# Last unit of a two-layer attention kernel: x and projection weights loaded ahead of its attention, range verdict ahead of the last evictions, general path out of line

## The chip, the cores and the metric

The kernel runs on one core of one Trainium2 chip, the seven other cores idle. The metric is the device time of one execution in microseconds (us). Before the change it is 3362.7 us, the median of 3 runs (3362.5 to 3364.94). The profiled execution took 3362.13 us, and its first to last instruction span 3360.4 us; times of single instructions below count from the start of that span.

## The reference

Two attention blocks of the same form follow each other, on 8 images of 512 channels and 32 x 32 = 1024 positions. All data is float32. One block, cut to what matters:

```python
xn  = groupnorm(x) * gn_scale + gn_bias            # 8 groups in block 0, 32 in block 1
qkv = einsum('oc,bcn->bon', qkv_w, xn) + qkv_b
q, k, v = split(qkv, 3)                            # 8 heads of 64 channels each
attn = softmax(einsum('bhdi,bhdj->bhij', q, k) / sqrt(64))
out = einsum('bhij,bhdj->bhdi', attn, v)
return einsum('oc,bcn->bon', proj_w, out) + proj_b + x
```

## The kernel before

**Units.** The work is cut into 16 units, one for each pair of block and image: units 0 to 7 are block 0, units 8 to 15 block 1. A unit `u` has four stages. Its x is loaded into the single buffer `xn` and normalised there. `projections` makes q, k and v. `attention` runs 64 steps, for 4 pairs of heads x 2 halves of the queries x 8 tiles of keys. The output projection of the unit is not run at once: `project(old, ...)` of unit `u - 1` comes between the projections and the attention of unit `u`. The products of `projections` and `project` are made in seven block products in place of eight (`blocks`, in the manner of Strassen), whose left and right operands are mixed ahead by `mix_weights` and `mix_right`. The last unit has no later unit to go into; it is projected plainly by `project_last`.

**The order of the work** is the order in which it is written (`tc.manual_schedule()`): each engine runs its own instructions in program order, and waits for the data and buffers that an instruction needs. All loads and stores are issued from SyncE's queue (SPq in the profile), also in program order, so an issue that waits for its buffer holds up all issues behind it.

**Attention.** Each step makes scores in PSUM (L486, TensorE, PE for short), takes the exponential on ScalarE (ACT, L494) into one of four shared buffers `p`, and multiplies it with v (L514). VectorE (DVE) adds the exponentials up (L531, L533), transposes and reduces these sums (L546, L556), and three small transfers gather them as `lt` (L562). `reciprocals` then takes the reciprocal, writes it to device memory (`drec`, L584) and reads it back spread over the partitions (`rb`, L589). `divide` multiplies the attention output `ao` by `rb` (L596), and `add_bias` adds the bias of v on ACT (L603). The output `ao` has four parts of 128 channels, one for each pair of heads. The fourth part is the last to be complete: for it these steps come after the attention, as `rest`.

**Buffers.** The residual of a unit (`load_res`) goes to the four buffers `p`, which the exponentials also use. The tags `w0`, `w1` and `w2` hold the mixed q, k and v weights of the block at hand.

**The last projection**, `project_last` (L430 to L454). The outputs lie in eight groups `g` (4 parts of 128 output channels x 2 halves of the positions), one PSUM bank each, taken from `turns`. First all groups get their products over parts 0, 1 and 2 of `ao` (24 products, each recorded as two matmul instructions of 512 columns). Then come the parts `rest` that complete part 3. Then each group gets its product over part 3, its eviction with the residual on DVE (L451) and its store (L454). Before the change the residual and the plain weights are loaded just ahead of this call, L728 and L729.

**The range verdict** (L733 to L741). The fast path takes the exponential without the maximum of a row being subtracted. Whether that was safe is recorded on the way, in `okay` and `asum`. At the end four DVE operations bring this down to one value on each partition (`both`), a product with ones adds up over the partitions, and the integer `flag` is written. Every engine loads the flag (L951) and branches (L952): if it is below 128, `general_path` computes everything again in a slow and safe way. With the inputs at hand it isn't entered. After the branch, L993 holds the end of the program, where all engines meet.

Of the kernel before, what the change touches and what calls it, by code (L numbers as in the profile page):

```python
# [11 lines left out]
F32 = mybir.dt.float32  # L12
I32 = mybir.dt.int32
AF = mybir.ActivationFunctionType
ALU = mybir.AluOpType
AX = mybir.AxisListType
DEP = mybir.DependencyInfo(mybir.DependencyClass.Sync, mybir.DependencyReason.DATA)

P = 128
# [13 lines left out]
def fast_path(ctx, tc, x, qkv_wT, proj_wT, vecs, groups, out, flag):  # L33
# [14 lines left out]
    nc = tc.nc  # L48
    B, C, N = x.shape
    CC = C // P  # L50
# [10 lines left out]
    def pool(name, bufs, **kw):  # L61
        return ctx.enter_context(tc.tile_pool(name=name, bufs=bufs, **kw))

    const = pool("const", 1)
# [11 lines left out]
    small = pool("small", 2)  # L76
# [7 lines left out]
    abank = [apair[i // 2][:, i % 2, :] for i in range(4)]  # L84

    turns = [t[:, i, :] for i in range(2) for t in (*sbank, *apair)]
# [3 lines left out]
    ones = const.tile([P, H], F32, name="ones")  # L90
    half = const.tile([P, CC], F32, name="half")
    okay = const.tile([P, 2 * BL], F32, name="okay")
    asum = const.tile([P, 2 * B * CC], F32, name="asum")
# [12 lines left out]
    def load_x(u, tiles):  # L106
        l, b = units[u]
        src = x[b] if l == 0 else mid[b]
        for c in range(CC):
            nc.sync.dma_start(tiles[c], src[c * P : (c + 1) * P, :])  # L110

    def load_xn(u):
        t = xnpool.tile([P, CC, N], F32, tag="xn", name=f"xn_{u}")
        load_x(u, [t[:, c, :] for c in range(CC)])
        return t

    def load_res(u):
        tiles = [ppool.tile([P, N], F32, tag="p", name=f"x_{u}_{c}") for c in range(CC)]
        load_x(u, tiles)
        return tiles  # L120
# [11 lines left out]
    def mix_weights(l, mats, engine, first=0):  # L132


        lefts, parts = [], []
        add, sub = engine.tensor_add, engine.tensor_sub
        for i, a in enumerate(mats, first):
            a11, a12 = a[:, :2, :FD2], a[:, 2:, :FD2]
            a21, a22 = a[:, :2, FD2:], a[:, 2:, FD2:]
            s1, s2, s4 = (  # L140
                wpool.tile([P, 2, FD2], F32, tag=f"s{k}w{i}", name=f"s{k}w{i}_{l}")
                for k in (1, 2, 4)
            )
            parts += [
                partial(add, s1, a21, a22), partial(sub, s2, s1, a11),
                partial(sub, a21, a11, a21), partial(sub, s4, a12, s2),
            ]
            lefts.append({1: a11, 2: a12, 3: s4, 4: a22, 5: s1, 6: s2, 7: a21})
        return lefts, parts

    def mix_right(name, low, high):


        b11, b12 = low[:, :, :FD], low[:, :, FD:]
        b21, b22 = high[:, :, :FD], high[:, :, FD:]
        t1, t2, t4 = (
            tpool.tile([P, 2, FD], F32, tag=f"{name[0]}{k}", name=f"{name}_t{k}")
            for k in (1, 2, 4)
        )
        sub = nc.vector.tensor_sub  # L160
        parts = (
            partial(sub, t1, b12, b11), partial(sub, t2, b22, t1),
            partial(sub, t4, b21, t2), partial(sub, b12, b22, b12),
        )
        return {1: b11, 2: b21, 3: b22, 4: t4, 5: t1, 6: t2, 7: b12}, parts

    def load_proj(l, tag):
        w = wpool.tile([P, CC, C], F32, tag=tag, name=f"wproj_{l}_{tag}")
        nc.sync.dma_start(w, proj_wT[l].rearrange("(c p) o -> p c o", p=P))
        return w  # L170
# [259 lines left out]
    def project_last(w, rest):  # L430

        l, b = units[w.u]
        dst = mid[b] if l == 0 else out[b]

        def products(g, c):
            o, h = divmod(g, NH)
            nc.tensor.matmul(  # L437
                turns[g], w.wproj[:, c, ts(o, P)], w.ao[c // 2][:, c % 2, ts(h, FD)],
                start=(c == 0), stop=(c == CC - 1),
            )  # L440

        for g in range(CC * NH):
            for c in range(CC - 1):
                products(g, c)
        for part in rest:
            part()
        for g in range(CC * NH):
            o, h = divmod(g, NH)
            products(g, CC - 1)
            cols = w.res[o][:, ts(h, FD)]  # L450
            nc.vector.scalar_tensor_tensor(  # L451
                cols, turns[g], vec[:, l, PB, o : o + 1], cols, ALU.add, ALU.add
            )
            nc.sync.dma_start(dst[o * P : (o + 1) * P, ts(h, FD)], cols)  # L454
# [205 lines left out]
    rest = {g: mixing_w[2 * i + 2 : 2 * i + 4] for i, g in enumerate((1, 3, 5, 8, 10))}  # L660
    rest[12] = mixing_o

    old = None
    for u in range(2 * B):
        w = Unit()
        w.u, w.right, w.lefts = u, right, lefts
        w.evac_before = []
        for part in mixing[2:]:
            part()
        if u == B + 1:  # L670
            rest[16] = mixing_o
        projections(w, rest)
        if old is not None:
            old.res = load_res(old.u)
        nxt = None
        if u + 1 < 2 * B:
            xn = load_xn(u + 1)
            nxt = norm_parts(u + 1, xn)
            right, mixing = mix_right(f"x_{u + 1}", xn[:, :2], xn[:, 2:])
        if u == B - 1:  # L680
            lefts, mixing_w = mix_weights(1, load_weights(1), nc.gpsimd)
            for part in mixing_w:
                part()

        def stats_of(*which):
            for i in which if nxt is not None else ():
                nxt[1](i // NH, i % NH)

        if old is not None:
            old.left = left_o  # L690
            stats_after = {3: (0, 1, 2), 4: (3,), 6: (4, 5), 7: (6, 7)}
            project(old, lambda g: stats_of(*stats_after.get(g, ())))
            w.evac_before = old.evac
            if old.u == B - 1:
                (left_o,), mixing_o = mix_weights(1, [load_proj(1, "wproj")], nc.vector, 3)


        late = 1 if u == 0 else 0

        def at_step(s, state):  # L700
            if nxt is None:
                return
            st, stats, aggregate, means, variances, scales, apply, _ = nxt
            c, t = divmod(s, NT)

            pair = (c + 1) % 2
            free = state["free"][pair]
            c -= late
            if u == 0 and NT // 2 <= s < NT:
                stats_of(2 * s - NT, 2 * s - NT + 1)  # L710
            if c == 1 and t == 1:
                aggregate()
            elif c == 1 and t == 3:
                means(abank[2 * pair], *free)
                free[:] = [st["last"]]
            elif c == 1 and t == 5:
                variances(abank[2 * pair], *free)
                free[:] = [st["last"]]
            elif c == 2 and t == 0:
                scales()  # L720
            elif 2 <= c < 2 + CC and t in (4, 6):
                apply(c - 2, int(t == 6))
            elif c == 2 + CC and t in (2, 5):
                mixing[int(t == 5)]()

        rest = attention(w, at_step)
        old = w
    old.res = load_res(old.u)  # L728
    old.wproj = load_proj(1, "w0")  # L729
    project_last(old, [part for g in (4, 10) for part in rest[g]])  # L730


    fin = small.tile([P, 2 * B * CC], F32, tag="fin", name="fin", bufs=1)  # L733
    nc.vector.tensor_scalar(fin, asum, 0.0, 0.0, ALU.mult, ALU.is_equal)
    low = small.tile([P, 2], F32, tag="low", name="low", bufs=1)
    nc.vector.tensor_reduce(low[:, 0:1], fin, AX.X, ALU.min)
    nc.vector.tensor_reduce(low[:, 1:2], okay, AX.X, ALU.min)
    both = small.tile([P, 1], F32, tag="both", name="both", bufs=1)
    nc.vector.tensor_mul(both, low[:, 0:1], low[:, 1:2])
    nc.tensor.matmul(abank[0][:1, :1], both, ones[:, :1], start=True, stop=True)  # L740
    nc.vector.tensor_copy(flag, abank[0][:1, :1])  # L741


def general_path(ctx, tc, x, qkv_wT, proj_wT, vecs, groups, out):
# [199 lines left out]
def attention_blocks_kernel(tc, x, qkv_wT, proj_wT, vecs, groups, out):  # L944
    nc = tc.nc
    with tc.tile_pool(name="flag", bufs=1) as keep:
        flag = keep.tile([1, 1], I32, name="flag")
        with ExitStack() as ctx:
            ctx.enter_context(tc.manual_schedule())
            fast_path(ctx, tc, x, qkv_wT, proj_wT, vecs, groups, out, flag)  # L950
        good = nc.values_load(flag[0:1, 0:1], min_val=0, max_val=P)  # L951
        with tc.If(good < P):  # L952
            with ExitStack() as ctx:
                general_path(ctx, tc, x, qkv_wT, proj_wT, vecs, groups, out)

# [49 lines left out]
```

## Time and profile before

| | |
|---|---|
| time, median of 3 | 3362.7 us |
| span of the profiled execution | 3360.4 us |
| PE busy (matmul) | 3316.9 us, 99% |
| VectorE busy | 2376.2 us, 71% |
| ScalarE busy | 1394.1 us, 41% |
| mean load on the memory | 44 GB/s |

How the stages around the change look, from the view that gives busy times by stretch:

| stretch, us from the start | what runs | PE busy | granted PE clock |
|---|---|---|---|
| 3098.2 to 3304.8 | last unit, up to the end of its attention | 206.59 | 1.00 |
| 3304.8 to 3322.8 | between attention and last projection | 0.01 | 0.57 |
| 3322.8 to 3345.9 | last projection, parts 0 to 2 | 23.10 | 0.89 |
| 3345.9 to 3353.0 | last projection, part 3 | 7.03 | 1.00 |
| 3353.0 to 3360.4 | verdict, branch, end | 0.19 | 0.63 |

The granted clock is the share of full speed that the chip gave TensorE. Busy time of PE is modelled from the ends of pipelined matmuls, so 99% doesn't say that its array is used at its peak. A row of the timeline or of the chain gives a start, a length and then the engine, the line of the kernel and the operation; what stands in brackets is how long the engine sat idle before it, and what released it. "SPq", "ACTq" and so on are the instruction queues of the engines, in which loads of registers, branches and semaphores show that don't count as busy.

### The profile page before, as it was taken

What the parts mean: (1) busy time and instruction counts of PE and PEld (TensorE: products, weight loads), DVE (VectorE), ACT (ScalarE), POOL (GpSimd) and SP (SyncE); (2) the same over time, 40 slices, a digit from 0 to 9 for tenths busy, and PEclk for the clock granted to TensorE, in tenths of its full rate; (3) what the DMA queues carried; (4) which work ended last, traced back from release to release, by engine and by line L of the source; (5) the groups of instructions that cost most, each with busy time, mean ns of one, the idle gap of its engine ahead of it and who ended that gap; (6) DMA issues with size and microseconds to landing.
All of it is one profiled execution on the core that took longest, in us unless ns stands there. A gap on an engine that the chain in (4) does not pass through costs nothing.

```text
span 3360.4 us, 51078 instructions
## 1 busy us (share of the span) xinstructions
PE 3316.9 (99%) x21002; PEld 1645.9 (49%) x21002; DVE 2376.2 (71%) x2978; ACT 1394.1 (41%) x1548; POOL 49.2 (1%) x32
## 2 busy tenths in 40 slices
PE   8999999999999999999999999999999999999996
PEld 4445454454545445454454544545445454454532
DVE  4876948668486785857859587594876948769484
ACT  1633606336172351724517154271542716336062
POOL 0000000000000000002000000000000000000000
PEclk9999999999999999999999999999999999999998
DMA  2011010110201111012120111101111010110102
GB/s 77 33 39 57 22 69 27 33 57 21 82 15 33 58 32 71 15 33 101 33 76 15 41 55 34 63 21 57 33 33 63 21 63 27 39 57 21 44 27 77
DMA packets 66845, 149.28 MB, mean 44 GB/s; under 512 B 20784, under 2 KB 21040, under 8 KB 66608
## 3 DMA queue, kind: packets, MB, share of 16 engines
q1 hardware_dynamic: 66608, 145.95, 13.1%
q8 instruction: 170, 2.79, 0.3%
q14 instruction: 67, 0.55, 0.1%
HBM read 110.26 MB, written 34.08 MB: 43 GB/s over the span
## 4 chain that ended last, share of the span: by engine, by line
PE 98%; DVE 1%; DMA 0%; issue 0%; SPq 0%; ACT 0%; POOL 0%; DVEq 0%
PE a L288 26%; PE a L514 26%; PE s L486 25%; PE s L288 19%; PE a L486 1%; PE s L437 0%; PE a L437 0%; DVE acc L533 0%; DMA wproj_w<-proj_wT_dram 0%; DMA xn<-x_dram 0%; DVE tr L546 0%; SPq L110 0%; PE a L196 0%; DVE red L556 0%; DVE acc L531 0%
## 5 line engine op out<-in xcount | busy, mean ns | idle before, releaser
L494 ACT ACTIVATE p<-s 128x1024 f32<-128x1024 f32 x976 | 998.3, 1024 | 815.8 <-PE s L486 781.8
L514 PE MATMUL a<-p,v 64*64 64x512 f32 x8192 | 1101.3, 589 | 0.1
L486 PE MATMUL s<-q,k 64*64 64x512 f32 x7808 | 1059.4, 590 | 1.4 <-DVE v L375 1.4
L533 DVE TENSOR_TENSOR acc<-acc,p 128x1024 f32<-128x1024 f32 x768 | 939.7, 1224 | 87.7 <-ACT p L494 39.6
L514 PEld LDWEIGHTS a<-p,v 64*64 64x64 f32 x8192 | 384.9, 131 | 494.4 <-ACT p L494 349.4
L486 PEld LDWEIGHTS s<-q,k 64*64 64x64 f32 x7808 | 385.8, 133 | 437.1 <-issue 434.6
L288 PE MATMUL a<-xn,w 128*128 128x512 f32 x512 | 233.4, 599 | 4.0 <-DVE xn L244 4.0
L531 DVE TENSOR_TENSOR acc<-p,p 128x1024 f32<-128x1024 f32 x128 | 153.7, 1201 | 12.9 <-ACT p L494 12.9
L288 PEld LDWEIGHTS a<-xn,w 128*128 128x128 f32 x512 | 96.6, 191 | 131.9 <-issue 127.4
L546 DVE STREAM_TRANSPOSE tr<-acc 128x1024 f32<-128x1024 f32 x128 | 158.0, 1235 | 0.0
L556 DVE TENSOR_REDUCE red<-tr 128x32 f32<-128x1024 f32 x128 | 153.9, 1202 | 0.6
L540 DVE TENSOR_TENSOR ao<-a,tmp 128x512 f32<-128x512 f32 x128 | 88.0, 688 | 68.8 <-ACT tmp L539 68.8
L300 ACT COPY p_k<-a 128x1024 f32<-128x1024 f32 x16 | 16.2, 1012 | 255.0 <-PE a L288 255.0
L300 ACT COPY p_o<-a 128x1024 f32<-128x1024 f32 x15 | 15.2, 1012 | 244.2 <-PE a L288 244.2
L288 PE MATMUL a<-w,xn 128*128 128x256 f32 x512 | 115.7, 379 | 0.0
L288 PE MATMUL s<-xn,w 128*128 128x512 f32 x256 | 115.2, 592 | 0.4 <-DVE u_q L304 0.4
L288 PE MATMUL s<-x_t,s2w 128*128 128x512 f32 x256 | 115.1, 592 | 0.0
L288 PE MATMUL a<-x_t,s1w 128*128 128x512 f32 x256 | 115.1, 592 | 0.0
L288 PE MATMUL s<-x_t,w 128*128 128x512 f32 x256 | 115.1, 592 | 0.0
L288 PE MATMUL a<-xn,s4w 128*128 128x512 f32 x256 | 115.1, 592 | 0.0
L300 ACT COPY p_v<-a 128x1024 f32<-128x1024 f32 x16 | 16.2, 1012 | 237.3 <-PE a L288 221.4
L288 PE MATMUL a<-ao,wproj_wproj 128*128 128x512 f32 x240 | 107.9, 592 | 0.0
(129 smaller groups left out, 2847.7 us busy)
## 6 DMA issues: line engine op xcount, KB each, us to landing
rb<-drec SPq DMA_DIRECT2D x128, 256.0 KB, 3.9
xn<-x_dram SPq DMA_DIRECT2D x32, 512.0 KB, 5.2
x<-x_dram SPq DMA_DIRECT2D x32, 512.0 KB, 4.6
mid<-x SPq DMA_DIRECT2D x64, 256.0 KB, 2.1
xn<-mid SPq DMA_DIRECT2D x32, 512.0 KB, 4.9
x<-mid SPq DMA_DIRECT2D x32, 512.0 KB, 5.0
out_dram<-x SPq DMA_DIRECT2D x64, 256.0 KB, 2.1
w<-qkv_wT_dram SPq DMA_DIRECT2D x6, 1024.0 KB, 11.5
```

The costliest lines, as they stand in the source:

```text
L288: nc.tensor.matmul(dst, at[:, c, ts(i, P)], moving[:, c, :], start=start and c == 0 and not (tokens and i % 2), stop=stop and c == 1, skip ...
L300: nc.scalar.copy(p1, bx)
L486: nc.tensor.matmul(bank[e * H : (e + 1) * H, j, :], w.k[pr][j * H : (j + 1) * H, t * P + e * H : t * P + (e + 1) * H], w.q[pr][j * H : (j ...
L494: exp = nc.scalar.activation(p, bank, AF.Exp, scale=SCALE)
L514: nc.tensor.matmul(banks[r][j * H : (j + 1) * H, :], w.v[rows, t, lo : lo + D], p[rows, j, :], start=(t == 0), stop=(t == NT - 1),)
L531: nc.vector.tensor_add(acc, state["first"], p)
L533: nc.vector.tensor_add(acc, acc, p)
L540: i1 = nc.vector.tensor_add(w.ao[pr // 2][:, pr % 2, ts(qh, FD)], banks[1], tmp)
L546: nc.vector.transpose(tr, state["acc"].pop(c))
L556: nc.vector.tensor_reduce(red[:, :, qh, :], state["tr"].rearrange("p j (f i) -> p j f i", i=BL), AX.X, ALU.add)
```

## The change

Three edits, all around the end of the kernel:

1. In the last unit there is no next x to load. Where other units load it, after their own projections, the last unit now loads its own x once more, into the same buffer `xn`, as the residual, and the plain projection weights into `w0`. The two loads ahead of `project_last` go.
2. The four DVE operations of the verdict become the last of the `rest` parts, ahead of the evictions of the last projection. The product with ones now goes to a bank of `turns`, and the flag is copied out by ScalarE instead of VectorE.
3. The branch on the flag is told that its body isn't the block to fall through to, so that the general path is laid out away from the straight path.

The aim is that PE finds its operands at the end of the attention, and that less is done in series after the last product.

```diff
             nxt = norm_parts(u + 1, xn)
             right, mixing = mix_right(f"x_{u + 1}", xn[:, :2], xn[:, 2:])
+        else:
+            again = load_xn(u)
+            w.res = [again[:, c, :] for c in range(CC)]
+            w.wproj = load_proj(1, "w0")
         if u == B - 1:
...
-    old.res = load_res(old.u)
-    old.wproj = load_proj(1, "w0")
-    project_last(old, [part for g in (4, 10) for part in rest[g]])
-
-    fin = small.tile([P, 2 * B * CC], F32, tag="fin", name="fin", bufs=1)
-    nc.vector.tensor_scalar(fin, asum, 0.0, 0.0, ALU.mult, ALU.is_equal)
-    low = small.tile([P, 2], F32, tag="low", name="low", bufs=1)
-    nc.vector.tensor_reduce(low[:, 0:1], fin, AX.X, ALU.min)
-    nc.vector.tensor_reduce(low[:, 1:2], okay, AX.X, ALU.min)
-    both = small.tile([P, 1], F32, tag="both", name="both", bufs=1)
-    nc.vector.tensor_mul(both, low[:, 0:1], low[:, 1:2])
-    nc.tensor.matmul(abank[0][:1, :1], both, ones[:, :1], start=True, stop=True)
-    nc.vector.tensor_copy(flag, abank[0][:1, :1])
+
+    both = const.tile([P, 1], F32, name="both")
+
+    def verdict():
+        fin = small.tile([P, 2 * B * CC], F32, tag="fin", name="fin", bufs=1)
+        nc.vector.tensor_scalar(fin, asum, 0.0, 0.0, ALU.mult, ALU.is_equal)
+        low = small.tile([P, 2], F32, tag="low", name="low", bufs=1)
+        nc.vector.tensor_reduce(low[:, 0:1], fin, AX.X, ALU.min)
+        nc.vector.tensor_reduce(low[:, 1:2], okay, AX.X, ALU.min)
+        nc.vector.tensor_mul(both, low[:, 0:1], low[:, 1:2])
+
+    project_last(old, [part for g in (4, 10) for part in rest[g]] + [verdict])
+    nc.tensor.matmul(turns[0][:1, :1], both, ones[:, :1], start=True, stop=True)
+    nc.scalar.copy(flag, turns[0][:1, :1])
...
-        with tc.If(good < P):
+        with tc.If(good < P, preferred_fallthrough_block=False):
```

## The prediction

> **What bounds the kernel now.** I read the page first, then the chain of waits. The page's chain puts the whole kernel on one engine:
>
> ```profile
> PE 98%; DVE 1%; DMA 0%; issue 0%; SPq 0%; ACT 0%; POOL 0%; DVEq 0%
> ```
>
> So an edit pays only where TensorE (PE) stands still, or after it has finished. The chain in order of time, asked for the last 65 us, has one such place; its columns are start, length (both us) and the piece:
>
> ```profile
> 3314.12 8.63 DMA wproj_w<-proj_wT_dram
> 3322.75 0.04 issue
> 3322.79 7.82 PE s L437 x12
> 3330.61 5.15 PE a L437 x12
> ```
>
> The last projection (L437) waits for a weight load that is issued when the attention is already over, and its first 12 matmul instructions take 7.82 us where the next 12 take 5.15. The timeline shows what the load queues behind and which work was ready long before:
>
> ```profile
> 3302.03 2.75 PE L514 MATMUL a<-p,v 64*64 64x512 f32 x24
> 3305.34 1.33 ACT L603 ACTIVATE ao<-ao,vec 128x512 f32<-128x512 f32 x2
> 3307.05 0.68 DVE L540 TENSOR_TENSOR ao<-a,tmp 128x512 f32<-128x512 f32 x1
> 3310.17 1.80 SPq L562 DMA_DIRECT2D lt<-red  x3
> 3312.08 1.94 SPq L110 DMA_DIRECT2D x<-mid  x4
> 3314.90 0.47 SPq L584 DMA_DIRECT2D drec<-rec  x1
> 3322.92 1.12 SPq L589 DMA_DIRECT2D rb<-drec  x2
> 3327.69 1.23 DVE L596 SCALAR_TENSOR_TENSOR ao<-ao,rb 128x1024 f32<-128x1024 f32 x1 [12.87 <-DMA rb<-drec]
> ```
>
> PE ends its attention products at 3304.78 and starts again at 3322.79: 18.0 us idle. On SyncE's queue (SPq) the x and weight loads stand behind the `lt` transfers of the denominators. `drec`, issued behind the weights at 3314.90, lands 8.0 us later (the page's DMA rows for all units: `rb` 3.9).
>
> The second place is after the last product, which ends at 3352.94. The flag is written at 3354.67 + 0.15 = 3354.82, but the span ends at 3360.4. The rows of the lines of the range test's branch (L952) and of the end (L993) give durations in ns and start times:
>
> ```profile
> L952 SPq EVENT_SEMAPHORE  x8: 17/17/17, 3356.2 to 3356.8; - x8
> L952 ACTq COMPARE_BRANCH  x1: 50/50/50, 3355.4 to 3355.4; - x1
> L952 PEldq COMPARE_BRANCH  x1: 3412/3412/3412, 3355.5 to 3355.5; - x1
> L952 ACTq EVENT_SEMAPHORE  x1: 17/17/17, 3358.9 to 3358.9; - x1
> L952 DVEq EVENT_SEMAPHORE  x1: 21/21/21, 3359.3 to 3359.3; - x1
> L993 SPq EVENT_SEMAPHORE  x10: 17/28/2254, 3356.8 to 3360.3; - x10
> ```
>
> PE sits 3.41 us in its branch; ScalarE (ACT) and VectorE (DVE) branch at 3355.4 and 3355.5 and do their next instruction at 3358.9 and 3359.3. SyncE, there at 3356.8, waits 2.25 us for them.
>
> [...] the first weight loads after the gap come 0.86 us apart, later ones 0.43; the price here is 7.82 − 5.15 = 2.67 us.
>
> **The change, part by part.**
>
> *Removed from the end: the x loads and the weight load.* The next thing PE can do after the attention is L437's first group. At the same place one unit earlier PE goes from its last x24 group at 3095.48 to 128*128 products at 3098.22, 2.74 us later, so the start becomes 3302.03 + 2.74 = 3304.77. Is its data there? The first four instructions (0.43 each) use `ao` parts finished long ago; the fifth, at 3306.49, needs the third part's bias, whose first half ends near 3305.34 + 0.66 = 3306.0. The second half and the `ao` of L540 (3307.73) are not needed before. This assumes waits by region, not by tile. At the start of the kernel, products on `xn` begin at 17.00 while other columns of `xn` are still written until 19.06, so regions it is. The start moves by 3322.79 − 3304.77 = 18.02 us, and with no idle window the 2.67 us of half clock go too: **20.7 us**. The 48 instructions then end at 3304.77 + 48 × 0.429 = 3325.4 (3346.06 before).
>
> *Does the last quarter wait instead?* Its chain starts with the `lt` transfers, unmoved. The third lands at 3313.18. Five small DVE operations follow, until 3314.5. `drec` goes out at once and takes 1.45 us with no weights ahead of it (mid-attention: issue 3268.37, `rb` issue 3269.82), so `rb` is issued at 3315.98. Issue to divide was 3327.69 − 3322.92 = 4.77, so divide runs 3320.75 to 3321.98 and the first half of the bias ends at about 3322.7. PE asks for it at 3325.4. Slack 2.7 us, cost nothing.
>
> *Added in the last unit: 2 MB of x and 1 MB of weights.* They stand on SPq behind the residual of the unit before. The x load needs the buffer `xn`, free when the V products end. The unit before does this with its own next load:
>
> ```profile
> 2964.03 1.75 SPq L110 DMA_DIRECT2D xn<-mid  x4
> 2975.11 14.60 SPq L411 DMA_DIRECT2D out_dram<-x  x8
> 3181.84 14.60 SPq L411 DMA_DIRECT2D out_dram<-x  x8
> ```
>
> The units are 3181.84 − 2975.11 = 206.73 apart, so x goes out at 3170.8, the weights at about 3172.6 for 0.69 us of issue; their buffer's last readers are the Q products (the first K product is already copied out at 3125.99). Queued behind them are the stores of L411, which begin at 3181.84; whoever needs those is the attention's exp, through the shared buffers. 3 MB at the 407 GB/s that the DMA view shows while the same loads run take 7.4 us, done near 3179, before the first store. Hidden behind 24 us of projection: nothing.
>
> *Verdict ahead of the evictions.* Four DVE operations (0.18 + 0.22 + 0.21 + 0.16) run at about 3322 to 3323, behind the divide, while DVE waits for PE: nothing. What waits behind them, the first eviction, needs a product of 3326.2. At the end there remain a matmul (0.20) and an ACT copy of one element; bounds for that are the DVE cast (0.15) and the ACT copy of 512 (0.58), I take 0.2.
>
> *Tail,* in before's clock. Flag at 3352.94 + 0.04 + 0.20 + 0.02 + 0.20 = 3353.4. DVE ends its last eviction at 3353.71, loads the flag (0.55) and branches by 3354.5. SyncE issues the last store until 3354.07 and takes 0.95 us for its flag load, check and branch as before (3354.8 to 3355.75): 3355.0. If the good path falls through, no engine fetches. Then the last store, issued 3353.73, lands 2.0 to 2.1 later, at 3355.8; SyncE's eight semaphore instructions cost 0 to 0.6 after it. From the last arrival to the end before took 3360.4 − 3359.3 = 1.1 us. New end: 3356.9 to 3357.5, **3.3 us** earlier (2.9 to 3.5).
>
> Sum: 20.7 + 3.3 = 24.0; 3362.7 − 24.0 = **3338.7 us**.
>
> **The rivals.**
>
> 1. *The fetch stays.* The new block order may only move the jump: a good path that is placed elsewhere, or must leap over the general path at the end. For it: the trace doesn't show the layout. Against: the name of the option says which side falls through. Then only the flag chain shortens: DVE branches at about 3354.4 in place of 3355.5, so 1.1 us in place of 3.3: 3362.7 − 20.7 − 1.1 = 3340.9.
> 2. *PE stops at the third part.* If the wait covers the whole `ao` tile, it lasts until L540, 3307.77 in place of 3306.49: 1.3 us, 3340.0. The regions at the start of the kernel speak against it.
> 3. *The denominator chain takes the weight load's place.* If it took 5 us more than worked out, the last quarter would wait 5 − 2.7 = 2.3 us: 3341.0. Without loads beside it, `rb` and `drec` have no reason to.
> 4. *Slower.* A buffer of the moved loads comes free only late in the last unit; SPq stands still, the stores behind go out late and the exps wait for their buffers. Held until the projection ends (3194.7), eight stores of 0.33 us and 2.1 of landing reach 3199.5, where the first exp started at 3195.85: some 4 us lost. With the weights also late, so that the 20.7 are not won, and a second fetch (3.4) on the way back from the moved block: 3362.7 + 4 + 3.4 = 3370. Unit 14's loads in the same place issue on time, which speaks against it.
>
> **Chances.** Forecast 0.68; fetch stays 0.18; third part 0.06; denominator chain 0.05; slower 0.02; within 0.2% (some 6.7 us) 0.01, since it needs most of the 18 us idle to survive. Faster 0.97. The range runs from the best tail with a microsecond of scatter, 3336.9, past rivals 1 to 3 to 3342.0.
>
> **What would show it.** Right: L437's first instruction within 2 us of 3304.8 and its first x12 near 5.2 us; no PE wait at the last quarter; PE's branch under 0.2 us; first store of the unit before still near 3181.8; span near 3336.4. Wrong: a PE wait for `ao` or for a DMA at L437, a branch of over 3 us on any engine, or an exp at 3196 that waits for a store.

## The result, and the profile after

The changed kernel takes 3341.79 us (median of 6 runs, 3340.12 to 3343.34) against 3362.94 us of the kernel before (6 runs). The ratio is 0.9936, with a 95% interval from 0.9923 to 0.9948: 21.2 us less, where 24.0 were forecast.

The profiled execution has a span of 3340.0 us, 20.4 less than before. The chain of waits of its last 50 us (start, length, piece) has no transfer in it any more:

```profile
3303.67 2.58 PE a L514 x24
3306.25 5.35 PE s L437 x12
3311.59 5.15 PE a L437 x12
...
3321.89 5.15 PE a L437 x12
3327.05 1.72 PE s L437 x4
...
3332.20 1.73 PE a L437 x4
```

The 8.63 us of the weight load have gone, and with them the first x12 of 7.82 us: it is 5.35 now. The timeline shows when the moved loads run, and that the denominators' chain has become free of them:

```profile
3172.22 1.75 SPq L110 DMA_DIRECT2D xn<-mid  x4
3174.06 0.49 SPq L169 DMA_DIRECT2D wproj_w<-proj_wT_dram  x1
3183.30 14.60 SPq L411 DMA_DIRECT2D out_dram<-x  x8
...
3303.49 2.75 PE L514 MATMUL a<-p,v 64*64 64x512 f32 x24
3306.18 5.42 PE L437 MATMUL s<-ao,wproj_w 128*128 128x512 f32 x12
3317.36 1.12 SPq L589 DMA_DIRECT2D rb<-drec  x2
3321.91 1.22 DVE L596 SCALAR_TENSOR_TENSOR ao<-ao,rb 128x1024 f32<-128x1024 f32 x1 [5.62 <-DMA rb<-drec]
3323.17 1.33 ACT L603 ACTIVATE ao<-ao,vec 128x512 f32<-128x512 f32 x2 [15.04 <-DVE ao L596]
```

The stores of the unit before begin 9.2 us after the weights are issued, with the same 14.60 us for the eight issues as before. Divide and bias are done before PE asks for the last quarter at 3326.88. The third part, too, is there in time. The first half of its bias (L603, 1.33 us for two) ends at about 3307.46 (estimate). PE's weight loads (PEld) of the first x12 go on in even steps across the one that waits for it, at 3307.57:

```profile
3306.80 1.33 ACT L603 ACTIVATE ao<-ao,vec 128x512 f32<-128x512 f32 x2
...
3307.14 0.19 PEld L437 LDWEIGHTS s<-ao,wproj_w 128*128 128x128 f32 x1 [0.24 <-issue]
3307.57 0.19 PEld L437 LDWEIGHTS s<-ao,wproj_w 128*128 128x128 f32 x1 [0.24 <-ACT ao L603]
3308.00 0.19 PEld L437 LDWEIGHTS s<-ao,wproj_w 128*128 128x128 f32 x1 [0.24 <-issue]
...
3308.51 0.68 DVE L540 TENSOR_TENSOR ao<-a,tmp 128x512 f32<-128x512 f32 x1
```

L540 writes another region of the same `ao` only later, and PE doesn't wait for that.

The branch (now L957) and the end (L998) look different from before, but not as forecast. Durations in ns, min/median/max, then first and last start:

```profile
L957 SPq EVENT_SEMAPHORE  x8: 17/17/17, 3336.1 to 3337.8; - x8
L957 ACTq COMPARE_BRANCH  x2: 38/44/49, 3334.8 to 3334.9; - x2
L957 PEldq COMPARE_BRANCH  x2: 95/1959/3823, 3334.8 to 3335.1; - x2
L957 DVEq COMPARE_BRANCH  x2: 51/55/59, 3334.9 to 3335.2; - x2
L957 SPq COMPARE_BRANCH  x2: 43/46/49, 3336.0 to 3337.9; - x2
L998 DVEq DRAIN  x2: 10/34/58, 3339.2 to 3339.6; - x2
```

Each engine now has two jumps. The first falls through (95 ns on PE). The second leads to the end of the program, over the general path, which still lies in between (the run with the short body below bears this out), and it takes PE 3.82 us, more than the 3.41 before. VectorE starts its second at 3335.2 and does its next instruction at 3339.2.

For comparisons two stretches are enough. **Stretch 1** goes from the start of the last x24 group of the attention to the end of the last product, **the tail** from there to the end of the span. Before: 3352.94 − 3302.03 = 50.91 and 3360.4 − 3352.94 = 7.46 us. After: 3333.93 − 3303.49 = 30.44 and 3340.0 − 3333.93 = 6.07 us. So stretch 1 gives 20.5 us and the tail 1.4, 21.9 together. That the profiled spans differ by 20.4 is due to 1.46 us that this execution lost long before the edits (the x24 group starts at 3303.49 in place of 3302.03); most of it, 1.04 us, went in its opening products, as the last section shows.

### The profile page after: what moved, and what is told of

It is laid out like the page before. It is cut to its first block, busy times and chain, and to the rows that moved or that the text cites. A ratio compares the mean times of both kernels' runs of the same rounds, so it can differ in the third digit from the quotient of the medians.

```text
span 3340.0 us, 51079 instructions
## 1 busy us (share of the span) xinstructions
PE 3315.5 (99%) x21002; PEld 1645.3 (49%) x21002; DVE 2375.6 (71%) x2977; ACT 1393.5 (42%) x1549; POOL 48.1 (1%) x32
## 4 chain that ended last, share of the span: by engine, by line
PE 98%; DVE 1%; issue 0%; DMA 0%; ACT 0%; POOL 0%; SPq 0%; DVEq 0%
PE a L514 26%; PE a L288 26%; PE s L486 25%; PE s L288 19%; PE a L486 1%; PE s L437 0%; PE a L437 0%; DMA xn<-x_dram 0%; DVE acc L533 0%; DVE x L422 0%; DVE stats L184 0%; PE a L196 0%; DVE tr L546 0%; DVE u_o L390 0%; POOL y L216 0%
## 5 line engine op out<-in xcount | busy, mean ns | idle before, releaser
L288 PE MATMUL a<-xn,w 128*128 128x512 f32 x512 | 234.4, 601 | 4.0 <-DVE xn L244 4.0
L288 PEld LDWEIGHTS a<-xn,w 128*128 128x128 f32 x512 | 96.9, 192 | 132.7 <-issue 128.1
L540 DVE TENSOR_TENSOR ao<-a,tmp 128x512 f32<-128x512 f32 x128 | 88.0, 687 | 69.9 <-ACT tmp L539 69.9
L300 ACT COPY p_o<-a 128x1024 f32<-128x1024 f32 x15 | 15.2, 1012 | 244.2 <-PE a L288 244.2
L288 PE MATMUL a<-w,xn 128*128 128x256 f32 x512 | 115.7, 379 | 0.0
L288 PE MATMUL s<-xn,w 128*128 128x512 f32 x256 | 115.2, 593 | 0.4 <-DVE u_q L304 0.4
L288 PE MATMUL s<-x_t,s2w 128*128 128x512 f32 x256 | 115.1, 592 | 0.0
L288 PE MATMUL a<-x_t,s1w 128*128 128x512 f32 x256 | 115.1, 592 | 0.0
L288 PE MATMUL s<-x_t,w 128*128 128x512 f32 x256 | 115.1, 592 | 0.0
L288 PE MATMUL a<-xn,s4w 128*128 128x512 f32 x256 | 115.1, 592 | 0.0
L288 PE MATMUL a<-ao,wproj_wproj 128*128 128x512 f32 x240 | 107.9, 592 | 0.0
```

The source lines that it names most:

```text
L288: nc.tensor.matmul(dst, at[:, c, ts(i, P)], moving[:, c, :], start=start and c == 0 and not (tokens and i % 2), stop=stop and c == 1, skip ...
L300: nc.scalar.copy(p1, bx)
L540: i1 = nc.vector.tensor_add(w.ao[pr // 2][:, pr % 2, ts(qh, FD)], banks[1], tmp)
```

## The experiments

Theory A, formed on this profile: the moved loads are nearly all of the gain, by an idle time and a half clock (granted 0.50 from 3323 to 3326 us before) that both go; the verdict gives about a microsecond; the layout only moves the jump, so that the end still waits for a far target. The rival B is the forecast: the layout takes the fetch away. Other rivals stand with each run. One table for all, each row from one profile and from the times of that kernel; each ratio is to the runs of the kernel before that stood beside it:

| kernel | stretch 1, us | tail, us | time, us | ratio to before, 95% interval |
|---|---|---|---|---|
| before | 50.91 | 7.46 | 3362.94 | |
| changed | 30.44 | 6.07 | 3341.79 | 0.9923 to 0.9948 |
| changed, once more | 30.44 | 6.20 | 3340.66 | 0.9917 to 0.9950 |
| loads only | 30.43 | 7.45 | 3342.44 | 0.9922 to 0.9955 |
| verdict only | 51.14 | 6.65 | 3362.09 | 0.9987 to 1.0005 |
| layout only | 51.22 | 7.57 | 3362.61 | 0.9990 to 1.0007 |
| changed without layout | 30.44 | 6.55 | 3341.08 | 0.9917 to 0.9950 |
| short body | 30.43 | 4.53 | 3338.88 | 0.9913 to 0.9946 |
| weights only early | 32.28 | 6.27 | 3343.48 | 0.9925 to 0.9958 |
| x only early | 45.59 | 6.30 | 3356.02 | 0.9970 to 0.9985 |
| before, PE kept busy | 48.34 | 8.14 | 3361.24 | 0.9985 to 1.0002 |
| hint | 30.43 | 6.57 | 3341.52 | 0.9919 to 0.9952 |
| block without hint | 30.43 | 6.56 | 3341.11 | 0.9917 to 0.9950 |
| late hint | 30.44 | 6.47 | 3341.70 | 0.9919 to 0.9953 |

The intervals are as wide as the effects of the two small edits, so those are judged by the tails of the profiles.

**One edit alone, and all but one.** The first three are the kernel before with one of the three edits of the diff above. Loads only:

> The first edit alone: x and projection weights of the last unit loaded ahead of its attention; verdict and branch as before. Theory A (the loads are nearly the whole gain, and the jump over the general path is only moved by the third edit): L437 starts 2.7 us after the last x24 attention group starts (20.8 us before), its first x12 takes 5.3 to 5.4 us, the tail from the last product to the end stays 7.5 us as before; in all 20.5 us less, about 3342.4 us. Theory B (as forecast, 3.3 of the gain belong to verdict and layout and the loads give 20.7): the same time for this run, since they differ only in the next three. Theory C (most of the idle time is replaced by another wait, for the bias or the denominators): a PE wait of several us at L437 and 3345 us or more.

Measured: L437 starts 2.69 us after the x24 group, stretch 1 is 30.43 and the tail 7.45. Expected by A and B; C, a new wait, is out. This edit alone is 20.5 us.

Verdict only:

> The second edit alone: four DVE operations of the verdict ahead of the last evictions, flag copied by ScalarE; loads late and branch as before. Theory A: the flag is written 1.4 us sooner after the last product (0.3 in place of 1.9 us), but VectorE is held by its last eviction and branches only 1.1 us sooner, so the tail shrinks from 7.5 to about 6.3 us and the time to 3361.7 us. Theory B: the same 1.1 us. Rival: the tail is set by the last store and doesn't move, 3362.9 us. The 18 us wait for the weights stays in every theory.

Measured: tail 6.65, so 0.8 in place of the 1.1 expected. The rows of its branch (L953) say why. VectorE branches at 3355.1, 1.05 us after the last product (3354.05) in place of 2.6, but then takes 4.6 us to its next instruction in place of 3.8; PE's jump too has become longer, 4.17 us:

```profile
L953 PEldq COMPARE_BRANCH  x1: 4172/4172/4172, 3355.0 to 3355.0; - x1
L953 DVEq COMPARE_BRANCH  x1: 76/76/76, 3355.1 to 3355.1; - x1
L953 DVEq EVENT_SEMAPHORE  x1: 21/21/21, 3359.7 to 3359.7; - x1
```

The last store also lands later there, 3.9 us after its issue in place of 2.1. Layout only:

> The third edit alone: general path not the block to fall through to; all else as before. Theory A (the branch on the flag now falls through, but is followed by a jump over the general path to the end, which waits for the same fetch): two branches on each engine, the second one of PE about 3.8 us long, VectorE and ScalarE reach the end 4 us after their jump, tail 7.5 to 7.9 us, time 3362.9 to 3363.3 us. Theory B (the fetch goes): no branch above 0.2 us, tail 5.3 us, time 3360.7 us.

Measured: two jumps on each engine, the second of PE 3.84 us; tail 7.57, no gain. B is out. The changed kernel without layout:

```diff
-        with tc.If(good < P, preferred_fallthrough_block=False):
+        with tc.If(good < P):
```

> The changed kernel without its third edit: loads and verdict moved, the general path in line again, so that the branch on the flag is taken. Theory A (the layout moves the jump and takes nothing away): one branch of about 3.4 us on PE, tail 5.9 to 6.3 us against 6.07 with the layout edit, time within 0.5 us of the changed kernel's 3341.8. Theory B (the layout edit still brings something): a tail of 7.5 us or more, 3343.5 us.

Measured: a jump of 4.25 us on PE, tail 6.55, slightly outside what A gave (5.9 to 6.3), far from B's 7.5. To see whether those 0.5 us are scatter, the changed kernel ran once more:

> The changed kernel once more, to see how far its tail of 6.07 us repeats, against 6.55 without the layout edit. If the layout edit brings half a microsecond together with the early verdict, the tail is again 6.0 to 6.2 us; if it was the scatter of one execution, it may lie at 6.3 to 6.7 us. The stretch from the last x24 group to the last product stays 30.4 us.

Its tail is 6.20. The four profiles with early verdict and the layout edit have 6.07, 6.20, 6.27 and 6.30 us, the three with early verdict and neither layout edit nor hint 6.55, 6.56 and 6.65. The groups don't overlap, so the layout edit seems to bring 0.3 to 0.4 us beside an early verdict; alone it brought none in the one profile (7.57 against 7.46). The times don't resolve it.

**Is the fetch what the tail waits for?** That a long jump waits for instructions to be fetched was the author's assumption in the prediction; the rows of the branch show only how long it takes. The general path replaced by two small transfers:

```diff
-                general_path(ctx, tc, x, qkv_wT, proj_wT, vecs, groups, out)
+                few = ctx.enter_context(tc.tile_pool(name="gfew", bufs=1))
+                t = few.tile([P, 4], F32, name="gt")
+                nc.sync.dma_start(t, vecs[:, :4])
+                nc.sync.dma_start(out[0, :P, :4], t)
```

> The changed kernel with the general path left out: the body of the branch holds only two small transfers, so that the jump over it is short. What it leaves out isn't entered with these inputs. Theory A (the fetch of a far jump target holds PE, VectorE and ScalarE at the end, and while it runs it also slows the last store): no branch above 0.3 us on any engine, the last store lands in 2.0 to 2.1 us in place of 2.7, tail 4.5 to 5.0 us against 6.07. Rival (the end is set by the meeting of the engines and the last store, the fetch lies beside them): long branches gone, tail still 5.8 us or more.

The same rows as above, of this kernel:

```profile
L957 PEldq COMPARE_BRANCH  x2: 90/135/180, 3332.5 to 3332.6; - x2
L957 DVEq COMPARE_BRANCH  x2: 51/55/59, 3332.6 to 3332.7; - x2
L1001 DVEq DRAIN  x2: 10/14/17, 3332.9 to 3335.6; - x2
L1001 SPq DRAIN  x3: 7/7/7, 3335.3 to 3335.6; - x3
```

All jumps are under 0.2 us, every store lands in 2.0 to 2.1 us, and the tail is 4.53: what is left is the last store and the meeting of the engines. The times agree: its slowest run, 3339.68 us, is under the fastest of the changed kernel, 3340.12. The fetch itself shows in the packets of the two queues that the pages call `q8 instruction` and `q14 instruction`. From the last product to the end, the kernel before moves two packets on q8 and six on q14, the changed one one and six. Over the whole execution every other kernel of the table moves 169 to 171 on q8 and 67 on q14, the one with the short body 168 and 61, so just six fewer on q14.

The far target costs 1.5 us of the changed kernel's tail, or somewhat more: with the short body SyncE also loads the flag and branches ahead of its last store, which goes out 1.4 us after the last product (3333.0) in place of 0.8 (3334.7 in the changed kernel). By the way it shows what the forecast of 3.3 us for the tail had described: 7.46 − 4.53 = 2.9.

**Which load, and what the half clock is worth.** Only the weights early, x late, against the changed kernel:

```diff
-            again = load_xn(u)
-            w.res = [again[:, c, :] for c in range(CC)]
             w.wproj = load_proj(1, "w0")
...
+    old.res = load_res(old.u)
     both = const.tile([P, 1], F32, name="both")
```

> The changed kernel with only the weights loaded ahead of the attention; the residual x is loaded late, as before. Theory A (the 18 us were the wait for the weights; x isn't needed before the evictions): L437 starts 2.7 us after the start of the last x24 group, as in the changed kernel. The reciprocals' transfer now stands behind 2 MB of x, lands about 16.3 us after that start, divide follows at 21.1 and the bias at 23.0, where the last quarter asks for it at 23.4: no wait or a few tenths, 3341.8 to 3342.3 us. Rival (the x load must go ahead too, since it holds up the denominators): the last quarter waits 2 us or more, 3344 us.

PE starts at once here too (2.68), so the weights were the whole wait at the start of L437. But the last quarter waits, by the timeline of this kernel:

```profile
3313.30 1.94 SPq L110 DMA_DIRECT2D x<-mid  x4
3315.76 0.32 SPq L584 DMA_DIRECT2D drec<-rec  x1
3321.66 1.12 SPq L589 DMA_DIRECT2D rb<-drec  x2
3326.34 1.23 DVE L596 SCALAR_TENSOR_TENSOR ao<-ao,rb 128x1024 f32<-128x1024 f32 x1 [10.29 <-DMA rb<-drec]
3328.39 1.98 PE L437 MATMUL s<-ao,wproj_w 128*128 128x512 f32 x4 [1.59 <-ACT ao L603]
```

`drec`, 8 KB, issued behind 2 MB of x, takes 5.9 us to land in place of the 1.4 that `rb`'s issue shows in the changed kernel; I had estimated that it lands 16.3 us after the x24 start, it was 18.4. Stretch 1 grows by 1.84 us. The rival that x must go ahead too is right, with its 2 us nearly reached.

Only x early, weights late:

```diff
-            w.wproj = load_proj(1, "w0")
...
+    old.wproj = load_proj(1, "w0")
     both = const.tile([P, 1], F32, name="both")
```

> The changed kernel with only x loaded ahead of the attention; the weights are loaded late, as before. Theory A: the weights go out about 10 us after the start of the last x24 group and, with no x ahead of them, land in 4.5 to 5.5 us instead of 8.6. L437 starts about 15 us after that start (20.8 before, 2.7 after), still at half clock in its first x12 (7.5 to 8.0 us); 5 to 6 us of the 20.5 are won, 3355 to 3356.5 us. Rival (x and weights share the gain evenly): L437 starts at 11 to 12 us, 3351 to 3353 us.

As A said: L437 starts 15.52 us after the x24 group and its first x12 takes 7.74 us:

```profile
3318.73 7.74 PE L437 MATMUL s<-ao,wproj_w 128*128 128x512 f32 x12 [12.77 <-DMA wproj_w<-proj_wT_dram]
```

The two loads don't share the gain: with x out of the way the weights still cost 45.59 − 30.44 = 15.2 us.

The kernel before, with products of no use in the idle stretch:

```diff
     old.wproj = load_proj(1, "w0")
+    for i in range(18):
+        nc.tensor.matmul(turns[0], left_o[1][:, 0, :P], old.ao[0][:, i % 2, :FD], start=True, stop=True)
```

> The kernel before, with 18 products of no use (two instructions of 0.43 us each, 15.4 us in all) on PE while it waits for the weights; their bank is overwritten afterwards. Theory A (part of the gain of the changed kernel, 2.6 us, is the half clock after the idle stretch): L437 starts as late as before, 20.8 us after the start of the last x24 group, but its first x12 takes 5.2 to 5.4 us in place of 7.8; the last product ends 2.5 us sooner, 3360.3 us. Rival (the slow first products come from the weights or from their first loads, not from the idle stretch): x12 stays at 7.8 us, 3362.9 us.

Measured:

```profile
3305.60 15.72 PE L731 MATMUL s<-ao,wproj_wproj 128*128 128x512 f32 x36
3323.52 5.42 PE L437 MATMUL s<-ao,wproj_w 128*128 128x512 f32 x12 [2.20 <-DMA wproj_w<-proj_wT_dram]
```

PE still waits for the weights until 20.6 us after the x24 start, but x12 is 5.42, and stretch 1 is 50.91 − 48.34 = 2.57 us shorter. Of these, 7.82 − 5.42 = 2.40 are the x12, and the rest is that the weights landed 0.16 us sooner after the x24 start (20.60 in place of 20.76). The weight loads of this x12 come 0.43 us apart from the start, where the first ones before came 0.86 apart at a granted clock of 0.50 (3323 to 3326 us); the mean clock of the profiled execution is 0.999 in place of 0.996. The idle stretch causes the slow products, and the 20.5 us split into 20.76 − 2.69 = 18.1 of waiting and 2.4 of half clock. The tail of this one is 8.14 us, since PE's jump takes 4.62; the length of that jump differs from program to program (3.41 to 4.62), and why is open.

**A version to beat both.** Can the far target be fetched ahead? Here a branch prefetch hint stands at the start of a block that holds the last projection:

```diff
-    project_last(old, [part for g in (4, 10) for part in rest[g]] + [verdict])
+    with tc.block():
+        tc.mark_branch_hint_location("skip", "LikelyTaken", engines=[mybir.EngineType.PE, mybir.EngineType.DVE, mybir.EngineType.Activation])
+        project_last(old, [part for g in (4, 10) for part in rest[g]] + [verdict])
...
-        with tc.If(good < P, preferred_fallthrough_block=False):
+        with tc.If(good < P, label="skip"):
```

> A version meant to beat both kernels: loads and verdict as in the changed kernel, the general path in line, and a prefetch hint for the far target of the branch on PE, VectorE and ScalarE. To place the hint, the last projection stands in a block of its own, at whose start each of the three engines meets the hint, some 27 us before the end on PE. Theory A (the end waits for the fetch of the target; fetched ahead it is gone): no branch above 0.5 us, the last store lands in 2.1 us, tail 4.5 to 5.0 us as with the short body, 3339 to 3340 us if the block costs nothing. Rival 1 (the hint is forgotten or has no effect): tail 6.1 to 6.6 us, 3341 us or more. Rival 2 (the start of a block makes engines meet, so that PE waits for VectorE's sums and the product start is lost again): L437 starts 6 us or more after the last x24 group's start in place of 2.7, 3344 us or more.

And the same block with the line of the hint left out, which has stretch 1 and tail as without a block, 30.43 and 6.56, so that the block is free:

> The same without the hint, to tell the cost of the block from the effect of the hint. Theory A: start of L437 as in the version with the hint, one branch of 3.4 to 4.3 us on PE, tail 6.1 to 6.6 us. If the block is free, 3341.1 us, as without block; if its start makes engines meet, later by that wait, the same in both versions.

With the hint the rows of the branch (L959) and of the end (L1000) read:

```profile
L959 ACTq COMPARE_BRANCH  x1: 68/68/68, 3332.9 to 3332.9; - x1
L959 PEldq COMPARE_BRANCH  x1: 415/415/415, 3333.0 to 3333.0; - x1
L959 DVEq COMPARE_BRANCH  x1: 89/89/89, 3333.1 to 3333.1; - x1
L959 ACTq EVENT_SEMAPHORE  x1: 17/17/17, 3335.8 to 3335.8; - x1
L959 DVEq EVENT_SEMAPHORE  x1: 21/21/21, 3337.6 to 3337.6; - x1
L1000 DVEq BRANCH_PREFETCH_HINT  x1: 56/56/56, 3308.5 to 3308.5; - x1
```

PE's jump falls from 4.18 us without the hint to 0.42: for PE the hint does fetch ahead. VectorE met its hint at 3308.5, yet it gets to the end 4.5 us after its jump, and since the slowest engine decides, the tail stays 6.57, as rival 1 said. A hint nearer to the jump was to tell whether VectorE had lost the target in between; there the block holds only the second loop of `project_last` (as `project_end`, not shown) and the flag. The diff is against the version above:

```diff
+    project_last(old, [part for g in (4, 10) for part in rest[g]] + [verdict])
     with tc.block():
         tc.mark_branch_hint_location("skip", "LikelyTaken", engines=[mybir.EngineType.PE, mybir.EngineType.DVE, mybir.EngineType.Activation])
-        project_last(old, [part for g in (4, 10) for part in rest[g]] + [verdict])
+        project_end(old)
```

> As the version with the hint, but the block with the hint holds only the last quarter of the projection, so that VectorE meets the hint some 11 us before its branch in place of 24, and ScalarE likewise. In the version before, the hint was met by all three engines and only PE's branch became short. Theory A (VectorE and ScalarE lost what they had fetched in between): VectorE reaches the end within 0.6 us of its branch, tail 4.5 to 5.2 us. Rival 1 (the hint has no lasting effect on these two engines wherever it stands): VectorE reaches the end 4 us after its branch, tail 6.1 to 6.6 us. Rival 2 (the start of this block makes PE wait for the parts before it): last product more than 30.9 us after the start of the last x24 group in place of 30.4.

VectorE met it at 3323.0, jumped at 3334.0 and was at the end at 3338.4: rival 1, 4.4 us again, tail 6.47. The DMA view says a little more. From 3325 us to the end the version with the late hint moves one q8 packet, where the changed kernel moves two, and six q14 packets, as the changed kernel does; over the whole execution the two move 170 and 169 on q8, and 67 on q14 each. That fits one fetch brought forward, PE's, while those of q14 were not; it looks less like a target that was lost again than like one that was never fetched ahead. The view doesn't say which engine a queue serves, so why the hint works on PE and not on VectorE and ScalarE stays open. Both versions beat the kernel before, but not the changed one.

## Why the prediction was right, and where it was off

The time was forecast as 3338.7 us; 3341.79 were measured, in the forecast direction and inside the range. The range held them by 0.2 us only, and because it had been drawn past the rivals, to 3342.0: what came true is the forecast for the loads together with rival 1 (3340.9) for the tail.

- *The loads, 20.7 us by the recorded sum.* Right: 20.5. The start was forecast 2.74 us after the x24 group and was 2.69; the half clock at 2.67 is worth 2.40. This term was sized too large by a reading: 7.82 us runs from the start of the first x12 to the end of its last product, while 5.15 is the distance from end to end in a stream that is already running. A first x12 at full clock takes 5.42 in the first of these views, in the changed kernel and in the one with PE kept busy. The bias of the third part costs nothing, as the PEld rows above show: waits go by region, as assumed. Rival 2 would have cost 1.3 us.
- *"Does the last quarter wait instead?"* Right: divide at 18.42 us after the x24 start (forecast 18.7), no PE wait. The run with x late shows how near the edge that is: 4.5 us more on one small transfer, and PE waited 1.6.
- *"Hidden behind 24 us of projection: nothing."* Right: the stores of the unit before begin at the same distance as before (3183.30 − 3172.22 = 11.08; 2975.11 − 2964.03 = 11.08 with one load fewer).
- *The tail, 3.3 us.* This step failed, in its words "If the good path falls through, no engine fetches", and by its own sign, "a branch of over 3 us on any engine". It does fall through, but the general path still lies between it and the end, so the next jump is the far one. That was rival 1, with 1.1 us for the tail; 1.4 were measured. I gave it too small a chance: that the trace doesn't show the layout was noted, and should have weighed more than the name of an option.
- *"the last store … lands 2.0 to 2.1 later".* Off: 2.7 in the changed kernel, 3.9 and 4.0 where the verdict is early without the layout edit. The store is late in just those runs whose far jump starts within a microsecond of its issue, and on time in the run with the short body and in those with the late verdict. That fetch and store hinder each other fits this and the longer jumps (4.17 and 4.25 us) in the same runs; it isn't shown by itself, and the longest jump, 4.62 us with PE kept busy, stands beside a store that was on time (SyncE's eight semaphore instructions behind it take 0.6 us, 3354.5 to 3355.1, as long as in the kernel before).

So 24.0 − 1.9 (tail) − 0.2 (half clock read too large) = 21.9, which is what the two stretches give. The rest, to the 21.2 of the medians, is no more than the scatter of the runs.

## What to carry to other kernels

Look at the last unit of a pipelined loop by itself: a load that every other unit issues early, because it is the next unit's, may have been left in front of its only user there, and the idle stretch of PE cost more than its length here: 18.1 us of waiting and 2.4 us of half clock. A small transfer on the critical chain should not be queued behind megabytes, even when the megabytes themselves are needed late: `drec` took 5.9 us in place of 1.4. For a rarely taken path it is not enough to be out of the branch's own way while the end of the program lies beyond it: the layout edit alone left the tail at 7.57 us, against 7.46. Whether a path placed behind the last instruction would cost nothing wasn't tried.

## What was not expected of the hardware

The same first products of the kernel (L288, 8 matmul instructions), ahead of any edit, take from 5.10 to 6.60 us in these 14 profiles, and start between 15.94 and 17.14 us. Their weight loads come first 0.86 us apart and then 0.43: in the kernel before (5.25 us for the eight) the slow spacing goes on until the load at 19.72 us, in the changed kernel (6.32 us) until the one at 22.25. The granted clock reads 1.00 in every microsecond from 17 to 23 us in both, so the half clock of the last projection is not seen here, and what spaces these loads is open. From the products that follow these to the last x24 group, all 14 profiles take 3279.9 to 3280.6 us, while the starts of that group lie 2.35 us apart. So the opening makes most of that difference between executions, and effects below a microsecond had to be read from stretches.

A flag that is known sooner needn't bring its full worth: with the early verdict alone, VectorE's jump came 1.5 us sooner after the last product, and the end only 0.8.
